# The loads of an exchange write every fourth partition instead of 32 neighbours, in a transformer block with expert routing

## The chip, the cores and the metric

The kernel runs on one core of one Trainium2 chip. Time is device time in microseconds (us) of the whole program on that core; smaller is better. A profile is one further execution, recorded by the hardware profiler.

## What is computed

The reference is one conditioned transformer block with expert-choice routing, in float32 throughout, for x of 16 sequences x 256 tokens x 256 features:

```python
shift = silu(t) @ W_ada.T + b_ada
h = ln(x, ln1_g, ln1_b) + shift
qkv = (h @ Wqkv.T).reshape(b, n, 3, H, HD)          # H = 16 heads, HD = 64
q = ln(qkv[:, :, 0].transpose(0, 2, 1, 3), qn_g, qn_b)
k = ln(qkv[:, :, 1].transpose(0, 2, 1, 3), kn_g, kn_b)
attn = softmax(einsum('bhnd,bhmd->bhnm', q, k) / sqrt(HD))
x = x + (attn @ v) @ Wout.T
gate = softmax(tok @ Wgate.T)                        # 4096 tokens, 8 experts
vals, idx = top_k(gate.T, 512)                       # each expert takes its 512 tokens
y = gelu(g @ fc1s + b1s) @ fc2s + b2s                # g: the tokens taken, layer-normed
tok = tok.at[idx].add(y * vals)
```

## The kernel before, in words

**Stages.** The program has an attention stage, in which the 16 sequences overlap like a pipeline (to about 800 us of the span), then a search for each expert's tokens, and then 16 expert jobs (8 experts, half of their tokens each). The change touches the attention stage alone.

**Order.** Each engine (TensorE = PE, VectorE = DVE, ScalarE = ACT, GpSimd = POOL, and the sync engine SP, which issues most DMAs) works through its own queue in order. The steps of the attention stage are declared with `plan.step` (lines 1330 to 1442), each with its engine, its assumed duration, what it needs and which buffers it holds. Their order does not come from those durations at build time: `plan.order(PLACES)` (line 1519) sorts them by a long list of places written out in the source (line 182). Semaphores then make each step wait for its data and its buffers.

**One sequence.** `First` norms the tokens and turns them into `hT`. `Group` (line 676) makes 512 columns of q, k or v for 128 tokens: `matmul` (688) into one of three PSUM buffers `pm`; for q and k `square` on ACT (701), `stats` on DVE (705), `power` on POOL (711 and 103), and `scale` on DVE (721), which empties `pm` into `qk` in SBUF. For v, ACT's `copy` (697) empties `pm`. `Quad` (line 796) does four heads, two at a time: `scores` (813) into two of four PSUM buffers `sc`, `maxima` on DVE (821), `exps` on ACT (830, one instruction for each 128 queries x 256 keys, with the row sum), `invert` on DVE (837), `normalise` on POOL (841), then the turned probabilities `prT` enter `product` (900), which ACT's `evict` (915) empties into `oT`. `Tail` (918) multiplies by Wout (926), adds x, stores, and computes the gates.

**The exchange.** q, k and the probabilities must be turned, so that what lay along the columns lies along the partitions. The first and the last sequence (`DIRECT`) do this with TensorE transposes. The other 14 do it in three steps. DVE transposes 32 x 32 blocks inside each group of 32 partitions (`turn`: line 754 for q and k into `kb`, line 851 for the probabilities into `pb`; two instructions of 128 x 512 fill one tile). SP then stores the whole tile of 512 KB to HBM in one DMA (`away`: 761 and 859). Last, SP loads it back in four DMAs of 128 KB (`back`: 773 and 873), each of which brings one 32-column block of all four partition groups to 32 partitions of the destination, in runs of 1 KB:

```python
for q in range(QB):                 # QB = 4, SQ = 32
    nc.sync.dma_start(
        prT[bass.ts(q, SQ)], self.blocks[i][:, :, q].rearrange("k m n -> m k n")
    )
```

So load q writes the 32 neighbouring partitions 32q to 32q + 31. For q and k, `affine` on ACT (781 and 789) then applies gain and bias. A sequence has 4 such round trips for q and k and 8 for the probabilities.

Of the kernel before, what the change touches and what calls it, by code (L numbers as in the profile page):

```python
# [12 lines left out]
AF = mybir.ActivationFunctionType  # L13
# [13 lines left out]
TB = N // P  # L27
# [7 lines left out]
SQ = 32  # L35
QB = P // SQ
# [28 lines left out]
def kernel(  # L65
# [105 lines left out]
    DIRECT = (0, B - 1)  # L171
# [356 lines left out]
    if True:  # L528
# [9 lines left out]
        xs, hTs, qTs, kTs, vs, oTs = {}, {}, {}, {}, {}, {}  # L538
# [134 lines left out]
        def plain(kT):  # L673
            return kT.rearrange("p g k t h m -> p (g k t h m)").rearrange("p (h n) -> p h n", n=N)

        class Group:
# [74 lines left out]
            def turn(self, kb):  # L751
                if self.t == 0:
                    kb.append(work.tile([P, QB, TB, HP // 2, SQ], F32, tag="pb", bufs=3, name="kb"))
                nc.vector.transpose(
                    kb[0][:, :, self.t],
                    self.qk.rearrange("p (h q d) -> p q h d", q=QB, d=SQ),
                )

            def away(self, kb):
# [6 lines left out]
            def back(self):  # L766
                if self.g < 2:
                    self.raw = work.tile([P, QB, TB, HP // 2, SQ], F32, tag="qraw", bufs=2, name="qraw")
                else:
                    self.raw = self.keys()[:, self.g - 2]  # L770
                raw = self.raw.rearrange("p k t h m -> p k (t h m)")
                for q in range(QB):
                    nc.sync.dma_start(
                        raw[bass.ts(q, SQ)], self.blocks[:, :, q].rearrange("k d n -> d k n")
                    )

            def affine(self):
# [18 lines left out]
        class Quad:  # L796
# [5 lines left out]
            def scores(self, i):  # L802
                hp = 2 * self.d + i
                direct = self.b in DIRECT
                keys = plain(kTs[self.b]) if direct else (
                    kTs[self.b].rearrange("p g k t h m -> p g h (k t) m")
                )
                for j in range(2):
                    self.sc[i, j] = ps.tile([P, TB, N], F32, tag="sc", bufs=4, name="sc")
                for t in range(TB):  # L810
                    for j in range(2):
                        rows = slice(j * HD, (j + 1) * HD)
                        nc.tensor.matmul(  # L813
                            self.sc[i, j][:, t, :], qTs[self.b][rows, hp, bass.ts(t, P)],
                            keys[rows, hp] if direct else keys[rows, hp // 4, hp % 4],
                            start=True, stop=True,
                        )
# [7 lines left out]
            def exps(self, i, j):  # L825
                if i not in self.sums:
                    self.sums[i] = stat.tile([P, 2, 2, TB], F32, tag="sums", name="sums")
                self.pr[i, j] = work.tile([P, TB, N], F32, tag="pr", bufs=PRB, name="pr")
                for t in range(TB):
                    nc.scalar.activation(  # L830
                        self.pr[i, j][:, t, :], self.sc[i, j][:, t, :], AF.Exp,
                        bias=self.nmax[i, j][:, t : t + 1], scale=1.0,
                        accum_out=self.sums[i][:, 0, j, t : t + 1],
                    )
# [34 lines left out]
            def back(self, i):  # L869

                prT = self.turned(i).rearrange("p (k n) -> p k n", k=QB)
                for q in range(QB):
                    nc.sync.dma_start(
                        prT[bass.ts(q, SQ)], self.blocks[i][:, :, q].rearrange("k m n -> m k n")
                    )

            def transposes(self, i, j):
# [472 lines left out]
        for b in range(B):  # L1350
# [16 lines left out]
            for (g, t), p in GROUP.items():  # L1367
                p += base
                a = Group(b, g, t)
                n = (b, g, t)  # L1370
# [27 lines left out]
            for d in range(HP // 2):  # L1398
                a = Quad(b, d)
                p = base + d * QUAD  # L1400
                g = d // 2
                n = (b, d)
                po = ("po", 0) + n
                for i in range(2):
                    q = p + 3 * i
                    m = n + (i,)
                    sums, pb, prT, blocks = ("sums",) + m, ("pb",) + m, ("prT",) + m, ("blocks",) + m
# [20 lines left out]
            for t in range(TB):  # L1428
                a = Tail(b, t)
                p = base + TAIL[t]  # L1430
                n = (b, t)
# [55 lines left out]
        for n in range(2):  # L1487
            a = jobs[n]
            k = top + 10 + 20 * n
# [19 lines left out]
        k = top + 30  # L1509
# [36 lines left out]
        for k in range(1, len(jobs)):  # L1546
# [4 lines left out]
            for s in range(SLOTS):  # L1551
# [28 lines left out]
                else:  # L1580
                    i, q = divmod(s - FC, 4)
# [56 lines left out]
```

## Time and profile before

| | us |
|---|---|
| median of 3 runs | 1095.7 (1095.66 to 1098.27) |
| the profiled execution | 1098.5, its span from first to last instruction 1096.8 |
| busy over the span | PE 1050.9 (96%), DVE 809.8 (74%), POOL 615.8 (56%), ACT 591.5 (54%) |
| busy from 100 to 750 us | PE 634.0, DVE 540.4, POOL 445.7, ACT 417.3, of 650 |
| DMA in the same stretch | 0.97 of the 16 DMA engines' time, 278 GB/s |

In the profile, L754 is line 754 of the kernel. A group of instructions is given as line, engine, operation, tile written <- tiles read, the shapes (partitions x elements), the number of instructions, then the busy time in us and the mean of one in ns, then the idle time that the engine had just before them and what ended it. A busy PE is not a PE at its peak, since the ends of matmuls are modelled; the spacing of their starts is the safer reading.

### The profile page before, as it was taken

How to read it: one execution, taken by the hardware profiler on the slowest of the kernel's cores; microseconds unless marked ns; L12 is line 12 of the kernel's file. 1: busy time of each engine (PE TensorE's matmuls, PEld its weight loads, DVE VectorE, ACT ScalarE, POOL GpSimd, SP SyncE). 2: the span in 40 equal slices, each digit the busy share in tenths (PEclk: the TensorE clock that was granted, in tenths of full speed). 3: DMA queues.
4: the chain of work that ended last, by engine and by line, in shares of the span. 5: the costliest groups of instructions: out<-in, count | busy, mean ns of one | idle time of the engine just before them, and what ended most of it. 6: DMA issues, size and time to landing. Idle time of an engine off the chain costs nothing. (4 is left out here: it accounts for less than half of the span.)

```text
span 1096.8 us, 18716 instructions
## 1 busy us (share of the span) xinstructions
PE 1050.9 (96%) x5611; PEld 685.9 (63%) x5611; DVE 809.8 (74%) x2257; ACT 591.5 (54%) x1656; POOL 615.8 (56%) x997
## 2 busy tenths in 40 slices
PE   6999999999999999999999999999988999999996
PEld 3555646556454645555565555656667888888885
DVE  6667878888887797887888788875579488655540
ACT  1768666666665655666666557675622323332331
POOL 3766766678667585666667676665411333333332
PEclk8999999999999999999999999999999999999998
DMA  6026989999998999998999999986120456565661
GB/s 213 1 77 188 273 261 294 285 281 261 282 278 269 282 280 284 283 286 255 281 294 275 285 283 266 310 265 186 64 101 20 132 172 202 169 174 171 194 202 19
DMA packets 167700, 238.56 MB, mean 218 GB/s; under 512 B 17328, under 2 KB 139440, under 8 KB 167600
## 3 DMA queue, kind: packets, MB, share of 16 engines
q1 hardware_dynamic: 159680, 227.08, 70.2%
q0 software_dynamic: 6144, 8.39, 4.2%
q10 hardware_dynamic: 1776, 1.90, 0.5%
q8 instruction: 45, 0.74, 0.3%
q14 instruction: 55, 0.45, 0.2%
HBM read 136.64 MB, written 100.66 MB: 216 GB/s over the span
## 5 line engine op out<-in xcount | busy, mean ns | idle before, releaser
L688 PE MATMUL pm<-wq,hT 128*128 128x512 f32 x768 | 361.5, 606 | 13.1 <-DVE qk L721 6.3
L841 POOL TENSOR_SCALAR pr<-pr,sums 128x256 f32<-128x256 f32 x512 | 237.0, 481 | 107.3 <-DVE sums L837 99.5
L830 ACT ACTIVATE pr<-sc,nmax 128x256 f32<-128x256 f32 x512 | 237.3, 481 | 98.3 <-DVE nmax L821 78.6
L688 PEld LDWEIGHTS pm<-wq,hT 128*128 128x128 f32 x768 | 136.8, 190 | 168.1 <-issue 131.6
L103 POOL TENSOR_TENSOR ss<-ss,neghalf 128x8 f32<-128x8 f32 x128 | 211.0, 1648 | 10.6
L821 DVE TENSOR_REDUCE nmax<-sc 128x2 f32<-128x512 f32 x256 | 165.4, 673 | 19.9 <-PE sc L813 19.6
L851 DVE STREAM_TRANSPOSE pb<-pr 128x512 f32<-128x512 f32 x224 | 150.1, 690 | 20.7 <-DMA kblocks<-kb 9.5
L813 PE MATMUL sc<-kT,qT 64*128 64x256 f32 x1024 | 137.4, 396 | 3.5 <-ACT kT L789 3.0
L900 PE MATMUL po<-prT,v 128*64 128x256 f32 x1024 | 129.5, 387 | 2.1 <-DMA prT<-blocks 1.8
L701 ACT ACTIVATE sq<-pm 128x512 f32<-128x512 f32 x128 | 75.8, 604 | 96.1 <-PE pm L688 95.6
L813 PEld LDWEIGHTS sc<-kT,qT 64*128 64x128 f32 x1024 | 91.9, 186 | 52.8 <-issue 26.7
L1319 POOL DMA_INDIRECT out<-y,idx x32 | 51.2, 1599 | 119.1 <-DVE y L1313 65.9
L1286 PE MATMUL ph<-xT,w 128*128 128x256 f32 x512 | 117.8, 383 | 0.0
L1302 PE MATMUL py<-w,hid 128*128 128x256 f32 x512 | 116.3, 380 | 0.0
L926 PE MATMUL pw<-wo,oT 128*128 128x256 f32 x512 | 115.3, 382 | 0.0
L926 PEld LDWEIGHTS pw<-wo,oT 128*128 128x128 f32 x512 | 96.2, 190 | 20.9 <-issue 6.0
L830 ACT ACTIVATION_READ_ACCUMULATOR pr<-sc,nmax 128x1 f32 x512 | 109.0, 213 | 0.0
L900 PEld LDWEIGHTS po<-prT,v 128*64 128x64 f32 x1024 | 66.8, 136 | 67.1 <-issue 23.7
L705 DVE TENSOR_REDUCE ss<-sq 128x8 f32<-128x512 f32 x128 | 85.1, 671 | 29.1 <-ACT sq L701 28.6
L1293 ACT ACTIVATE hid<-ph,vec 128x256 f32<-128x256 f32 x128 | 60.3, 473 | 84.6 <-PE ph L1286 79.5
L1302 PEld LDWEIGHTS py<-w,hid 128*128 128x128 f32 x512 | 95.6, 190 | 12.8
L1286 PEld LDWEIGHTS ph<-xT,w 128*128 128x128 f32 x512 | 95.4, 190 | 12.8
(141 smaller groups left out, 1096.1 us busy)
## 6 DMA issues: line engine op xcount, KB each, us to landing
blocks<-pb SPq DMA_DIRECT2D x112, 512.0 KB, 5.0
prT<-blocks SPq DMA_DIRECT2D x448, 128.0 KB, 4.3
kblocks<-kb SPq DMA_DIRECT2D x56, 512.0 KB, 4.3
w<-in_fc2T SPq DMA_DIRECT2D x16, 1024.0 KB, 5.7
w<-in_fc1T SPq DMA_DIRECT2D x16, 1024.0 KB, 8.3
qraw<-kblocks SPq DMA_DIRECT2D x112, 128.0 KB, 4.0
kT<-kblocks SPq DMA_DIRECT2D x112, 128.0 KB, 4.2
out<-tok SPq DMA_DIRECT2D x32, 128.0 KB, 4.1
```

What stands on the lines that cost most here:

```text
L103: nc.gpsimd.tensor_tensor(dst, src, neghalf[:, : src.shape[1]], ALU.pow)
L688: nc.tensor.matmul(self.pm, hTs[self.b][:, c, bass.ts(self.t, P)], wq[:, c, bass.ts(self.g, GW)], start=(c == 0), stop=(c == DC - 1),)
L705: nc.vector.tensor_reduce(self.ss[:, 0, :], self.sq.rearrange("p (h d) -> p h d", d=HD), AX.X, ALU.add,)
L813: nc.tensor.matmul(self.sc[i, j][:, t, :], qTs[self.b][rows, hp, bass.ts(t, P)], keys[rows, hp] if direct else keys[rows, hp // 4, hp % 4] ...
L821: nc.vector.tensor_reduce(self.nmax[i, j], self.sc[i, j], AX.X, ALU.max, negate=True)
L830: nc.scalar.activation(self.pr[i, j][:, t, :], self.sc[i, j][:, t, :], AF.Exp, bias=self.nmax[i, j][:, t : t + 1], scale=1.0, accum_out=se ...
L841: nc.gpsimd.tensor_scalar(self.pr[i, j][:, t, :], self.pr[i, j][:, t, :], self.sums[i][:, 1, j, t : t + 1], 1.0, ALU.mult, ALU.mult,)
L851: nc.vector.transpose(self.pb[i][:, :, :, j].rearrange("p k c t n -> p t k c n"), self.pr[i, j].rearrange("p t (k c m) -> p t k c m", c=TB ...
L900: nc.tensor.matmul(self.po[j * HD : (j + 1) * HD, i, :], vs[self.b][:, c, bass.ts(4 * self.d + 2 * i + j, HD)], prT[:, j, c] if self.b in ...
L926: nc.tensor.matmul(self.pw, oTs[self.b][:, hp // 2, self.t, hp % 2, :], wo[:, hp, :], start=(hp == 0), stop=(hp == HP - 1),)
L1286: nc.tensor.matmul(self.ph[f], self.w1[:, c, bass.ts(f, P)], self.xT[:, c, :], start=(c == 0), stop=(c == DC - 1),)
L1302: nc.tensor.matmul(self.py[i], self.hid[:, f, bass.ts(i, P)], self.w2[:, f, :], start=(f == 0), stop=(f == FC - 1),)
```

## The change

Load q writes partitions q, q + 4, q + 8, ... q + 124. For the data to land where it did, block q must hold every fourth column instead of 32 neighbouring ones. For q and k, DVE's transpose (754) reads its source with a step of four elements, 16 bytes. For the probabilities, ACT's exponential reads the scores from PSUM with that step and writes them to SBUF in block order without gaps, so that `normalise` and DVE's transpose (851) are as before. The matmul of the scores now takes the keys in their natural order, still in runs of 32 neighbouring elements. The DIRECT sequences, the stores, the number, sizes and queues of the DMAs, and the order of every queue are as before.

```diff
@@ Group.turn
                 nc.vector.transpose(
                     kb[0][:, :, self.t],
-                    self.qk.rearrange("p (h q d) -> p q h d", q=QB, d=SQ),
+                    self.qk.rearrange("p (h d q) -> p q h d", q=QB, d=SQ),
                 )
@@ Group.back
                     nc.sync.dma_start(
-                        raw[bass.ts(q, SQ)], self.blocks[:, :, q].rearrange("k d n -> d k n")
+                        raw[q::QB], self.blocks[:, :, q].rearrange("k d n -> d k n")
                     )
@@ Quad.scores
                 keys = plain(kTs[self.b]) if direct else (
-                    kTs[self.b].rearrange("p g k t h m -> p g h (k t) m")
+                    kTs[self.b].rearrange("p g k t h m -> p g h t k m")
                 )
@@ Quad.exps
                 for t in range(TB):
+                    dst, src = self.pr[i, j][:, t, :], self.sc[i, j][:, t, :]
+                    if not (self.b in DIRECT):
+                        dst = dst.rearrange("p (q c m) -> p q c m", q=QB, c=TB)
+                        src = src.rearrange("p (c m q) -> p q c m", q=QB, c=TB)
                     nc.scalar.activation(
-                        self.pr[i, j][:, t, :], self.sc[i, j][:, t, :], AF.Exp,
+                        dst, src, AF.Exp,
@@ Quad.back
                     nc.sync.dma_start(
-                        prT[bass.ts(q, SQ)], self.blocks[i][:, :, q].rearrange("k m n -> m k n")
+                        prT[q::QB], self.blocks[i][:, :, q].rearrange("k m n -> m k n")
                     )
```

## The prediction

> **What bounds it now.** I read the busy times by stretch first, then TensorE's own waits, then the DMA. From 100 to 750 us the attention stage runs evenly:
>
> ```profile
> core 0: us, PE busy (x) PEld busy (x) DVE busy (x) ACT busy (x) POOL busy (x), PEclk, DMA share, GB/s
> 100.00:750.00 650.00, 633.98 (x3069) 360.00 (x3069) 540.39 (x1077) 417.34 (x1248) 445.70 (x773) 1.00 0.97 278
> ```
>
> Two things look full: PE (98%) and the DMA engines (0.97). DVE is at 83%, ACT at 64%. As a busy PE may be a waiting one, I took the spacing of matmul starts in the trace and counted what exceeds the usual spacing of each pair of lines. Stalls of over 0.15 us sum to 18.2 us from 100 to 770 us. So PE bounds the stage, and whatever speeds up everything else can win some 18 us. Following each stall back through its releases, 11 of the 25, worth 8.0 us, begin at the landing of a DMA. The rest come from DVE's and ACT's queues. PE's waits in that stretch show the same pattern:
>
> ```profile
> engine line waited for: us in total, times, longest us
> PE pm L688 <- DVE qk L721: 3.1, 6, 1.0
> PE sc L813 <- ACT kT L789: 3.0, 3, 1.9
> PE pm L688 <- ACT v L697: 2.8, 2, 1.6
> ...
> PE po L900 <- DMA prT<-blocks: 1.8, 3, 1.4
> ```
>
> The product waits for its loads (L900) only 1.8 us in all. DMA is full, but PE hardly feels it.
>
> **What the loads cost now.** A stretch with stores only, then one with loads only, then stores again:
>
> ```profile
> 404.75:405.75 1.00, 1.00 (x6) 0.90 (x5) 1.00 (x2) 1.00 (x5) 0.92 (x2) 1.00 0.94 345
> ...
> 406.50:409.75 3.25, 3.25 (x14) 1.86 (x14) 3.04 (x9) 1.52 (x2) 3.07 (x8) 1.00 1.10 225
> 410.75:411.75 1.00, 0.00 (x0) 0.00 (x0) 0.84 (x2) 0.69 (x1) 0.70 (x2) 1.00 1.04 375
> ```
>
> The last two columns are DMA share and GB/s: loads move 225, stores 345 to 375, both with all engines busy. In the packet records of the loads a 1 KB packet takes mostly 70 to 90 ns, while undisturbed ones take 46. So something makes the loads wait on each other, and 32 neighbouring partitions are a plausible something. Had every 1 KB packet its 46 ns, then from 300 to 350 us (7004 of them, 468 us over 16 engines, 29.2 us each) an engine would spend 20.1 us: 9 of 50 us are freed, a DMA share near 0.8. One load of four has 512 packets, 32 an engine; at 34 ns less each it lands 1.1 us sooner.
>
> **Gain.** If each of the 11 stalls shrinks by up to 1.1 us, 6.8 of the 8.0 us go. I take **-7 us**. What is late next is the queues of DVE and ACT, whose stalls (10 us) stay.
>
> **Costs.** Nothing is reordered, and no DMA or wait is added: the queues hold the same steps, so nothing moves past another. Two kinds of instruction get a 16-byte step in what they read:
>
> ```profile
> L830 ACT ACTIVATE pr<-sc,nmax 128x256 f32<-128x256 f32 x512 | 237.3, 481 | 98.3 <-DVE nmax L821 78.6 <-POOL pr L841 8.3 <-POOL ss L103 5.6
> ...
> L754 DVE STREAM_TRANSPOSE kb<-qk 128x512 f32<-128x512 f32 x112 | 77.6, 697 | 6.5 <-DMA blocks<-pb 5.6
> ...
> L1172 DVE TENSOR_SCALAR partf<-pplace 128x256 f32<-128x256 f32 x2 | 0.9, 426 | 4.1 <-PE pplace L1161 4.1
> ...
> L998 DVE TENSOR_TENSOR gate_of<-gates,smax 128x224 f32<-128x224 f32 x1 | 0.7, 744 | 0.0
> ...
> L1034 DVE COPY gates<-pgT 128x256 f32<-128x256 f32 x1 | 0.4, 414 | 0.0
> ...
> L990 DVE TENSOR_TENSOR gates<-gates,smax 128x224 f32<-128x224 f32 x1 | 0.4, 392 | 0.0
> ```
>
> The trace has no read at 16 bytes. The nearest rows bracket it. L1172 writes with a step of 8 bytes and takes 426 ns, against 414 for the gapless copy L1034: free. L998 writes with a step of 128 bytes: 744, against 392 for L990 of the same form, so 1.57 ns more for each of 224 elements. So an element costs 0 to 1.57 ns more, and both rows are writes of DVE; for ACT's read of PSUM they are a distant bound. A gain is excluded: the same elements go through. I take one cycle of DVE, 1.03 ns (from 679 ns for the 512 elements of L721 and 415 for the 256 of L933), and as much for ACT by its own pace (0.83 ns, from 594 for 512 and 380 for 256 in its copies). This is a choice near the middle, not a measurement.
>
> DVE: a transpose goes from 697 to about 1230 ns, 112 x 0.53 = 59 us. ACT: an exponential goes from 481 to about 694, 448 (14 sequences) x 0.213 = 95 us. From 100 to 750 us (102 and 448 of them) DVE would be busy 540 + 54 = 594 of 650 us (91%), ACT 513 (79%). Neither passes PE, so most of it is hidden under the matmuls. But the queues are in order: behind a late transpose stand `scale` (L721), which frees PE's `pm`, and `maxima` (L821), for which ACT and then PE's `sc` wait. For the share that reaches PE I followed the releases back from PE's last work before 765 us to 100 us by the rule of the chain of waits (the page's own chain ends at once in POOL's queue). On that path lie 357 us of PE, 127 of DMA, 93 of DVE, 29 of ACT. L754 has 11.3 us there, 16% of its transposes, and the exponentials 11.8 us, 5.5% of theirs. Present shares give 59 x 0.16 + 95 x 0.055 = 9.5 + 5.2 us. As DVE's idle time halves (110 to 56 us) and ACT's falls from 233 to 137, delays are absorbed less: shares of 33% and 9.5% give 19.6 + 9.1 us. I take the middle, **+15 and +7 us**.
>
> The Trainium skill bears on this choice: "SBUF — State Buffer", section "Door 1: The DMA port swizzle", says that SBUF is read at full rate only with at least two hits in each 16-byte line, and that PSUM's lines are 8 bytes. The rows L1172 (8 bytes, two hits) and L998 (one) agree. By it a 16-byte step is slowed on both engines, which speaks against the change; without a slowdown the sum would be the -7 alone.
>
> At nothing: the scores' new key order. Its inner runs are 32 elements before and after, and the DIRECT sequences, which read keys without gaps, have the same 376 ns median of L813. If it did cost, PE would show it at once: 896 matmuls, 0.01 us each is 9 us. The exponential still writes without gaps, so `normalise` and the 224 transposes of L851 stay at 481 and 690 ns.
>
> **Sum.** -7 + 15 + 7 = +15 us. On the profiled execution's 1098.5 us (span 1096.8, with 1.7 around it) that is 1113.5; it lies 2.8 above the median, so for the median **1111 us**.
>
> **Rivals.**
>
> *Strided reads are free* (0 ns an element, as at 8 bytes). Then only the gain is left: 1089, at best 1084 if some stalls in DVE's queue came from the DMA too, at worst 1092. For it: L1172. Against it: L998.
>
> *DVE becomes the bound.* At 1.57 ns an element the transposes take 1.5 us: 540 + 102 x 0.80 = 622 of 650 us, and ACT 417 + 448 x 0.40 = 597. DVE now waits 110 us, 27 of it for DMAs; if the other 83 stay, it needs 705 us, PE starves for `pm`, and the stage is 55 us longer: 1151. It decides once DVE's work and the waits it can't lose pass 650 us, that is beyond about 0.27 us more for each transpose if none of those 83 us can be lost, and beyond 1.1 us if all can. Against it: much of DVE's waiting is slack that a later DVE simply uses up.
>
> *It cancels*: only one engine is slowed, or the loss hides under PE, and the sooner loads pay for the rest: 1093 to 1098.
>
> *The change doesn't do what it says*: engines still meet in pairs at the same place, since each writes two of the 32 partitions in turn, and loads stay near 225 GB/s. With the slow reads that is +22 us, 1118; it lies inside the forecast's range.
>
> **How the numbers follow.** Forecast (slow reads, partly hidden; with or without quicker loads), 1099 to 1135: 50%. Free reads: 25%. Cancelled: 14%. DVE the bound, 1135 to 1175: 11%. A measurement here can tell 0.3%, 3.3 us, from no change. Faster takes the free reads, 25%; no change 14%; slower 61%. The range from 1088 to 1142 leaves out the lowest third of the free reads' times and most of the DVE-bound case. The forecast's own is 1099 to 1135.
>
> **What would show it.** L754's mean: 1230 ns right, 700 wrong, 1500 for the DVE-bound rival; L830's: 690 against 481. Loads-only stretches above 300 GB/s, 1 KB packets near 46 ns and a DMA share near 0.8 show the gain's cause. PE's waits for L721, L697 and L830 should grow, and those for kT and prT shrink. The prediction is wrong if the strided rows keep their time, or if they slow and PE's stalls stay at 18 us.

## The result, and the profile after

The changed kernel takes 1134.4 us (median of 4 runs, 1132.9 to 1136.0), the kernel before 1095.7 on the same chip: a ratio of 1.034, with a 95% interval from 1.032 to 1.036. It is slower by 3.4%, some 37 us, where +15 us had been forecast. One of the runs further below, of `e2_qk_only`, took 2129 us, is counted as slow, and is left out of its ratio.

Three groups and a queue of the profile page after come first. The columns of a group are line, engine, operation, tiles, shapes and count, then busy us and mean ns of one, then idle us before it and what ended most of it. Below 830 the line numbers have moved by four: L834 was L830, L855 was L851, L877 was L873.

```profile
q1 hardware_dynamic: 159680, 227.08, 59.6%
...
L834 ACT ACTIVATE pr<-sc,nmax 128x256 f32<-128x256 f32 x512 | 237.6, 481 | 125.0 <-DVE nmax L821 101.9
...
L855 DVE STREAM_TRANSPOSE pb<-pr 128x512 f32<-128x512 f32 x224 | 150.0, 691 | 27.0 <-DMA kblocks<-kb 10.2
...
L754 DVE STREAM_TRANSPOSE kb<-qk 128x512 f32<-128x512 f32 x112 | 123.3, 1105 | 5.4 <-DMA blocks<-pb 4.7
```

DVE's strided transpose went from 697 to 1105 ns. ACT's strided exponential did not move at all: 481 before, 481 after. The queue q1 carried the same 159680 packets and 227 MB in 59.6% of the DMA engines' time, against 70.2% before:

```profile
q1 hardware_dynamic: 159680, 227.08, 70.2%
```

The stretch from 100 to 750 us, with two shorter stretches from inside it, by the view of busy times (the last three columns are granted clock, DMA share and GB/s):

```profile
100.00:750.00 650.00, 613.84 (x2898) 345.13 (x2897) 551.77 (x1028) 393.93 (x1173) 422.54 (x732) 0.99 0.79 265
343.00:351.00 8.00, 6.57 (x26) 3.10 (x27) 6.72 (x14) 4.58 (x13) 3.62 (x4) 0.79 0.75 226
422.50:424.50 2.00, 2.00 (x11) 1.74 (x11) 2.00 (x6) 1.99 (x6) 1.62 (x2) 1.00 0.77 202
```

Every engine but DVE is busy for less of it than before (PE 614 against 634), and DVE is at 552 of 650: none of the five is full any more. The DMA share fell from 0.97 to 0.79, as forecast. But the third line is a stretch with loads only, and they move 202 GB/s, less than the 225 of before, at a share of 0.77. Now it isn't the packets that are slow: for a quarter of that stretch the DMA engines have nothing to do. The stretch is a usual one: over all stretches of 1.5 us or more without a packet of 2 KB or larger, from 100 to 750 us, the median is 227 GB/s at a share of 0.98 before (66 stretches), and 208 at 0.69 after (72).

The last matmul of Wout (L930 after) starts at 843.4 us instead of 808.8; what follows takes 288 to 289 us in both. So the whole loss, 34.6 us between the two profiled executions, lies in the attention stage. Counted as the prediction counted them, PE's stalls there rose from 18.2 us (25 of them) to 47.1 (54). What PE waits for is a new list (100 to 780 us):

```profile
engine line waited for: us in total, times, longest us
PE pl L967 <- ACT oT L919: 12.0, 5, 3.9
PE po L904 <- DMA prT<-blocks: 5.1, 4, 2.3
PE pm L688 <- DVE qk L721: 4.7, 8, 1.1
PE pm L688 <- ACT hT L659: 3.3, 1, 3.3
```

The first row is the tail of a sequence. Its gates (L967) wait behind the last evicted product, and a product waits for its loads. Its stalls are few and long: 12 us in five.

The view that explains them is SP's own instructions: duration in ns, min/median/max of one DMA issue. First before, then after:

```profile
L873 SPq DMA_DIRECT2D prT<-blocks x440: 302/430/1713, 105.0 to 747.4; - x147
```

```profile
L877 SPq DMA_DIRECT2D prT<-blocks x408: 577/602/1812, 106.1 to 748.5; - x136
L773 SPq DMA_DIRECT2D qraw<-kblocks x104: 577/602/1262, 109.4 to 743.9; - x104
```

Issuing one stepped load holds SP's queue for 602 ns, where a load to neighbours took 302 at best and 430 in the median. From the start of one load to the start of the next of the same four, the median is 0.647 us instead of 0.48. SP issues DMAs for 514 of the 650 us (79%), against 410 (63%) before. And 131072 bytes every 0.647 us are 203 GB/s: the stretch of loads alone showed 202.

### The profile page after: what moved, and what is told of

It reads as the page before. It is cut to its first block, busy times and chain, and to the rows that moved or that the text cites. A ratio compares the mean times of both kernels' runs of the same rounds, so it can differ in the third digit from the quotient of the medians.

```text
span 1131.5 us, 18747 instructions
## 1 busy us (share of the span) xinstructions
PE 1062.7 (94%) x5611; PEld 689.8 (61%) x5611; DVE 849.4 (75%) x2257; ACT 591.7 (52%) x1656; POOL 617.0 (55%) x997
## 3 DMA queue, kind: packets, MB, share of 16 engines
q1 hardware_dynamic: 159680, 227.08, 59.6%
## 5 line engine op out<-in xcount | busy, mean ns | idle before, releaser
L688 PE MATMUL pm<-wq,hT 128*128 128x512 f32 x768 | 366.2, 611 | 18.9 <-DVE qk L721 7.9
L834 ACT ACTIVATE pr<-sc,nmax 128x256 f32<-128x256 f32 x512 | 237.6, 481 | 125.0 <-DVE nmax L821 101.9
L855 DVE STREAM_TRANSPOSE pb<-pr 128x512 f32<-128x512 f32 x224 | 150.0, 691 | 27.0 <-DMA kblocks<-kb 10.2
L813 PE MATMUL sc<-kT,qT 64*128 64x256 f32 x1024 | 140.8, 398 | 2.7 <-ACT kT L789 2.1
L754 DVE STREAM_TRANSPOSE kb<-qk 128x512 f32<-128x512 f32 x112 | 123.3, 1105 | 5.4 <-DMA blocks<-pb 4.7
L930 PE MATMUL pw<-wo,oT 128*128 128x256 f32 x512 | 115.3, 382 | 0.3 <-DVE qk L721 0.3
L930 PEld LDWEIGHTS pw<-wo,oT 128*128 128x128 f32 x512 | 96.2, 190 | 21.2 <-issue 4.9
L834 ACT ACTIVATION_READ_ACCUMULATOR pr<-sc,nmax 128x1 f32 x512 | 108.2, 211 | 0.0
```

The costliest lines, as they stand in the source:

```text
L688: nc.tensor.matmul(self.pm, hTs[self.b][:, c, bass.ts(self.t, P)], wq[:, c, bass.ts(self.g, GW)], start=(c == 0), stop=(c == DC - 1),)
L754: nc.vector.transpose(kb[0][:, :, self.t], self.qk.rearrange("p (h d q) -> p q h d", q=QB, d=SQ),)
L813: nc.tensor.matmul(self.sc[i, j][:, t, :], qTs[self.b][rows, hp, bass.ts(t, P)], keys[rows, hp] if direct else keys[rows, hp // 4, hp % 4] ...
L834: nc.scalar.activation(dst, src, AF.Exp, bias=self.nmax[i, j][:, t : t + 1], scale=1.0, accum_out=self.sums[i][:, 0, j, t : t + 1],)
L855: nc.vector.transpose(self.pb[i][:, :, :, j].rearrange("p k c t n -> p t k c n"), self.pr[i, j].rearrange("p t (k c m) -> p t k c m", c=TB ...
L930: nc.tensor.matmul(self.pw, oTs[self.b][:, hp // 2, self.t, hp % 2, :], wo[:, hp, :], start=(hp == 0), stop=(hp == HP - 1),)
```

## The experiments

Each ratio is to the kernel before on the same chip; "us" behind it is that ratio on 1095.7 us. In the first four, two theories stood against each other. **Q**: the loss is DVE's slower transposes, late in an in-order queue. I believed this one first, since following PE's last work back through the releases put 235 of 698 us on DVE, against 93 of 665 before. **L**: the loss comes with the stepped loads. The last four set **S** (issuing a stepped load holds SP's queue longer) against what was left of L.

**Only the probabilities' half of the change** (`e1_probs_only`): q and k are turned and loaded as before.

```diff
 # against the changed kernel
-                    self.qk.rearrange("p (h d q) -> p q h d", q=QB, d=SQ),
+                    self.qk.rearrange("p (h q d) -> p q h d", q=QB, d=SQ),
...
-                        raw[q::QB], self.blocks[:, :, q].rearrange("k d n -> d k n")
+                        raw[bass.ts(q, SQ)], self.blocks[:, :, q].rearrange("k d n -> d k n")
```

> The changed kernel with the q/k part undone: line 754 reads neighbours again and its loads write 32 neighbours; the probabilities keep the strided exponentials and the spread loads. Theory Q (the loss is DVE's 112 strided transposes, 46 us of DVE time, which an in-order queue hands on to PE almost whole): the loss is gone and the sooner loads are left, 1088 to 1096 us, L754 back at about 700 ns. Rival L (the loss comes from the loads landing sooner in an order written for slower ones, or from the probabilities' new path): slower than before by 10 us or more, 1106 to 1130.

Measured: 1115.1 us, ratio 1.014 (1.012 to 1.016), +15 us. No instruction of DVE is strided here, and 448 of the 672 loads are stepped. By Q there should have been no loss.

**Only the q and k half** (`e2_qk_only`): the two edits above, made the other way round in the kernel before.

> The kernel before with only the q/k part of the change: strided transposes at line 754 and spread q/k loads; the probabilities as before. Theory Q: nearly the whole loss, with less of the loads' relief, 1128 to 1142 us. Rival L: most of the loss is missing, 1096 to 1112.

Measured: 1110.2 us, ratio 1.009 (1.006 to 1.012), +10 us. The whole of DVE's slow work is in this kernel, with 224 stepped loads, and together they cost a quarter of the loss. The two halves make 15 + 10 = 25 us apart and 37 together, so the cost is not in proportion to the number of loads; the row at the end of this section takes that up.

**The stepped loads alone** (`e3_loads_alone`): nothing is read with a step; only the destinations change.

```diff
 # against the kernel before
-                        raw[bass.ts(q, SQ)], self.blocks[:, :, q].rearrange("k d n -> d k n")
+                        raw[q::QB], self.blocks[:, :, q].rearrange("k d n -> d k n")
...
-                        prT[bass.ts(q, SQ)], self.blocks[i][:, :, q].rearrange("k m n -> m k n")
+                        prT[q::QB], self.blocks[i][:, :, q].rearrange("k m n -> m k n")
```

> The kernel before with only the loads spread over every fourth partition and no strided read; so the rows of q, k and the probabilities land in the wrong partitions, while every instruction has its usual size. Theory Q: faster by what the stalls that begin at a landing hold, at most 8 us: 1088 to 1095. Rival L: slower, 1105 to 1130.

Measured: 1127.6 us, ratio 1.026 (1.024 to 1.029), +29 us. The busy view of this kernel:

```profile
100.00:750.00 650.00, 617.40 (x2908) 347.33 (x2910) 518.11 (x1034) 397.20 (x1179) 424.50 (x735) 0.98 0.79 266
```

DVE is the least loaded of all versions so far (518 of 650), DMA is at 0.79, and the kernel is 29 us slower. So Q falls as the explanation of the whole.

**The strided reads alone** (`e4_strides_alone`): the same two lines, put back in the changed kernel.

> The changed kernel with its strided reads but the loads to 32 neighbours as before; so rows land in the wrong partitions. Theory Q: the loss without the relief, 1134 to 1150 us. Rival L: near the kernel before, 1096 to 1112.

Measured: 1108.2 us, ratio 1.008 (1.006 to 1.010), +9 us. With 29 from the loads that makes 38, against 37 for the change: the two parts add up.

**Each exchange loaded by one DMA** (`e5_one_load`). With the step, the 128 destination partitions run through the four blocks in one regular order, so the four loads can be one of 512 KB.

```diff
 # against the changed kernel
-                for q in range(QB):
-                    nc.sync.dma_start(
-                        prT[q::QB], self.blocks[i][:, :, q].rearrange("k m n -> m k n")
-                    )
+                nc.sync.dma_start(prT, self.blocks[i].rearrange("k m q n -> (m q) k n"))
 # and the same for raw
```

> The changed kernel with each four loads of an exchange joined in one DMA: with every fourth column in a block, 128 partitions in their order are one source step in HBM, so one load of 512 KB does what four of 128 KB did. Theory S (a load to every fourth partition holds SP's queue for 602 ns at the median instead of 430, 0.17 us more for each of 672, and the in-order queue hands that on): SP's issuing falls from 514 us (100 to 750 us) to under 200, the loads' loss goes, and only the strided transposes' 9 us is left, less what sooner loads can win: 1094 to 1108 us. Rival L (loads that land sooner upset the rest, or take something from the engines): still 1120 to 1140 us, as the loads land sooner still.

Measured: 1091.1 us, ratio 0.997 (0.996 to 0.998), -3.5 us, below even the 1094 to 1108 that S expected: SP's queue is freer now than it was before the change. The same bytes land in the same places, DVE's transposes are as slow as in the change, and the loss is gone. SP's issues and the largest of SP's waits, in this kernel:

```profile
L873 SPq DMA_DIRECT2D prT<-blocks x111: 359/374/1330, 106.8 to 745.5; - x111
```

```profile
SPq L860 <- DVE pb L852: 120.4, 64, 6.8
```

One load of 128 partitions is issued in 374 ns, where a quarter of it took 602. SP issues for 170 of 650 us and spends most of the rest waiting for DVE's data; before and in the change its largest waits were for the probabilities' stores to land:

```profile
SPq L873 <- DMA blocks<-pb: 65.4, 44, 5.3
SPq L877 <- DMA blocks<-pb: 26.2, 16, 3.8
```

In the change steps whose data was ready stood behind SP's issues, and the traces show it directly. Taken in order, each store of the probabilities belongs to two transposes of DVE. From the end of the second one to the issue of the store, the median of the 112 is 1.2 us before, 2.6 in the change, 2.8 in `e3_loads_alone` and 0.03 here. The same loads-only reading in this kernel, from 424.25 to 428.50 us:

```profile
424.25:428.50 4.25, 4.25 (x14) 1.97 (x12) 3.51 (x7) 2.27 (x6) 2.98 (x7) 1.00 0.95 291
```

291 GB/s at a share of 0.95, now that the engines get their work in time. It is one of the fuller ones: the median of all such stretches in this kernel is 240 GB/s at 0.79.

**The same, and the step moved to a read of PSUM** (`e6_one_load_psum`): `scale` reads `pm` with the step and writes `qk` gapless in block order; the transpose then reads without a step.

```diff
 # against the changed kernel, besides the edit of the one load
                 engine.tensor_tensor(
-                    self.qk.rearrange("p (h d) -> p h d", d=HD),
-                    src.rearrange("p (h d) -> p h d", d=HD),
-                    self.ss[:, 1, :].unsqueeze(2).to_broadcast([P, 8, HD]), ALU.mult,
+                    self.qk.rearrange("p (q h d) -> p q h d", q=QB, h=8),
+                    src.rearrange("p (h d q) -> p q h d", q=QB, h=8),
+                    self.ss[:, 1, :].unsqueeze(1).unsqueeze(3).to_broadcast([P, QB, 8, HD // QB]),
+                    ALU.mult,
                 )
...
-                    self.qk.rearrange("p (h d q) -> p q h d", q=QB, d=SQ),
+                    self.qk.rearrange("p (q h d) -> p q h d", q=QB, d=SQ),
```

> As the one with joined loads, and the strided read moved from DVE's transpose (L754, SBUF) to DVE's scaling (L721), which reads the matmul's result in PSUM in block order and writes without gaps. If DVE reads PSUM with a 16-byte step as freely as ACT did, L721 stays at 680 ns and L754 goes back to 700: theory S says 1085 to 1096 us, below the kernel before; rival L 1112 to 1132. If DVE pays in PSUM as in SBUF (about 0.4 us), it equals the one with joined loads, 1094 to 1108.

Measured: 1078.3 us, ratio 0.985 (0.983 to 0.986), -17 us: faster than both kernels, and below the 1085 to 1096 expected. DVE's groups and the busy view of it:

```profile
L762 DVE STREAM_TRANSPOSE kb<-qk 128x512 f32<-128x512 f32 x112 | 77.2, 694 | 0.8
L728 DVE TENSOR_TENSOR qk<-pm,ss 128x512 f32<-128x512 f32 x112 | 75.8, 679 | 16.2 <-POOL ss L103 14.5
```

```profile
100.00:750.00 650.00, 650.00 (x3198) 374.39 (x3195) 551.48 (x1100) 430.94 (x1275) 454.81 (x789) 1.00 0.82 282
```

The transpose is back at 694 ns, and `scale`, which now reads PSUM with a step of 16 bytes, takes the 679 that it took without one. PE is busy in all 650 us. By the count of stalls over 0.15 us it has none. The 17 us won are nearly the 18.2 us of PE's stalls that the prediction called the most there was to win.

**Does the step make the issue long, or the busier queue?** (`e7_steps`): in the kernel before, q's loads write every second partition of 64, k's every fourth, and the probabilities' stay at neighbours.

```diff
 # against the kernel before
+                    two = bass.ds(q // 2 * 64, 64)
+                    dst = raw[two][q % 2 :: 2] if self.g < 2 else raw[q::QB]
                     nc.sync.dma_start(
-                        raw[bass.ts(q, SQ)], self.blocks[:, :, q].rearrange("k d n -> d k n")
+                        dst, self.blocks[:, :, q].rearrange("k d n -> d k n")
                     )
```

> The kernel before with other destinations of the q and k loads: q every second partition of 64, k every fourth of 128, the probabilities still 32 neighbours; q and k rows land in wrong partitions. One look, for the time that SP's queue is held by each kind of issue. Theory S: k loads about 602 ns at the median and the probabilities 430 in the same run; q shows whether any step costs this or only the fourth. Rival: all three kinds take the same, so that the longer issues belong to a busier queue and not to the step. Time near 1105 to 1112 us.

Measured, in one execution: 1098.6 us. Before's own profiled execution, on another chip, took 1098.5, and ten runs of before on this chip 1092.6 to 1097.0, with a median of 1094.6; so 0 to 4 us for 224 stepped loads, less than the 1105 to 1112 expected. SP's issues, all in one execution:

```profile
L775 SPq DMA_DIRECT2D qraw<-kblocks x104: 572/602/1753, 107.7 to 709.5; - x104
L775 SPq DMA_DIRECT2D kT<-kblocks x104: 577/604/1927, 112.3 to 717.5; - x104
L875 SPq DMA_DIRECT2D prT<-blocks x440: 302/430/1740, 105.1 to 747.6; - x147
```

On one queue, mixed together, the stepped ones take 602 and 604 and the others 430. It is the step, of two as of four, and not the load on the queue.

**A longer issue without any step** (`e8_sp_drains`): the kernel before, with an instruction on SP behind each load that only holds its queue, four times.

```diff
 # against the kernel before, after each of the two loads
+                    for _ in range(4):
+                        nc.sync.drain()
```

> The kernel before with four drain instructions in SP's queue after each of the 672 loads, and nothing else changed, to hold the queue longer while every transfer stays as it was. Theory S: if the four hold SP for about as long as the step of four partitions did (0.17 us), the time rises by 15 to 35 us, to 1113 to 1134; if they hold it for 0.05 us, by 3 to 10. Rival L: no change, whatever they hold, 1095 to 1101.

Measured: 1138.6 us, ratio 1.041 (1.039 to 1.043), +44 us, above the 1113 to 1134 expected. The four held SP for 0.21 us a load by the spacing (0.69 against 0.48), more than the step's 0.17. A store of the probabilities now stands 3.0 us in the median behind its data. With the data, the work of DVE and ACT, and the destinations all as before, delay in SP's queue alone makes the loss of the change and more.

The runs make a row: extra time on SP's queue against time lost. Extra is 0.167 us for each stepped load, 0.21 for each load with drains.

| kernel | loads lengthened | extra on SP, us | lost, us |
|---|---|---|---|
| `e7_steps` | 224 | 37 | 0 to 4 |
| `e1_probs_only` | 448 | 75 | 15 |
| `e3_loads_alone` | 672 | 112 | 29 |
| `e8_sp_drains` | 672 | 141 | 44 |

The first 40 us or so vanish in SP's idle time. Of what comes on top, a third to a half reaches the end. The row mixes number with kind: the 224 are all q's and k's loads, the 448 all the probabilities'. The first three kernels also have the destinations that make packets quicker, and `e8_sp_drains` has not. These were not separated. Nor did I try one load for the kernel before: with neighbours, the source of a joined load needs one dimension more.

## Why the prediction was wrong, point by point

**The step that failed** is the sentence "Nothing is reordered, and no DMA or wait is added: the queues hold the same steps". It holds for order and number. But it passes off each of the 672 loads as the same instruction, with no price for the issue itself, which is 0.17 us longer. On SP's in-order queue that is 112 us, in a queue that was issuing for 63% of the stage and waited at its head for stores to land for another 65 us, by SP's waits. The cost is +29 us (e3), with the step as the cause of the long issue (e7) and the long issue as a sufficient cause of the loss (e8), and it goes when the issues go (e5). The prediction gave a price to DVE and ACT, and none to the queue that the edit itself was in. Yet the path that it followed back from PE's last work holds 18.6 us of SP's queue before, which it did not list beside PE, DMA, DVE and ACT; in the change it is 39.6. A row to bound the cost was there, too: the trace of before has issues of one form of load from 302 to 1713 ns, with 430 in the median, so 672 loads at 0.1 us more, 67 us, would have raised the question of what SP's idle time can absorb.

**DVE's transposes**: forecast 1230 ns and +15 us. Measured 1105 ns (0.80 ns more an element, from 408 ns over 512), and +9 us in e4. With SP relieved, e5 against e6, taking the stride away is worth 13 us. The slow read was right, and its price a little high. (The larger of its two shares comes to 31 to 32% by its own numbers, 16% x 110 / 56, and not 33%; that takes half a microsecond off the 15.)

**ACT's exponentials**: forecast 694 ns and +7 us. Measured 481 ns and nothing. The choice "near the middle" of 0 and 1.57 ns was wrong: two rows of DVE's writes to SBUF said nothing of a read of PSUM. The Trainium skill ("SBUF — State Buffer", section "Door 1: The DMA port swizzle") has lines of 16 bytes for SBUF, with two hits in a line needed for full rate, and lines of 8 bytes for PSUM, where it speaks of matmuls alone. The transpose agrees with it. The prediction carried the rule over to what engines read from PSUM, and the exponential (481 and 481) and `scale` in e6 (679 and 679) do not follow it: neither ACT nor DVE lost anything with a step of 16 bytes in PSUM.

**The quicker loads**: the signs came, and the cause is only in part shown. 1 KB packets take 46 ns in the median and 53 in the mean (from 300 to 350 us; 67 in the mean before), the DMA share is 0.79 for "near 0.8", and a load of the probabilities lands 3.1 us after its issue instead of 4.3, 1.2 us sooner for the 1.1 worked out (that is the sum for the four loads of a tile, which have 512 packets; one load has 128). These are the page's rows, with KB and us to landing, first the probabilities' before and then after:

```profile
prT<-blocks SPq DMA_DIRECT2D x448, 128.0 KB, 4.3
```

```profile
prT<-blocks SPq DMA_DIRECT2D x448, 128.0 KB, 3.1
...
qraw<-kblocks SPq DMA_DIRECT2D x112, 128.0 KB, 3.0
kT<-kblocks SPq DMA_DIRECT2D x112, 128.0 KB, 3.3
```

But e8, whose loads go to 32 neighbours and are only issued more slowly, shows much of the same: packets of 46 ns in the median and 57 in the mean, and a DMA share of 0.83. So a part of the relief is the slower pace itself. That the destination counts too is seen in e5, where SP's issuing no longer sets the pace, the destination is all 128 partitions, and a full stretch of loads still moves 291 GB/s, against 225 before, with packets of 46 and 52 ns.

And landing is counted from the issue, while the fourth issue now comes 3 x 0.167 = 0.5 us later, behind every other delay of the queue. The sign "loads-only stretches above 300 GB/s" failed for the same reason: 202, the pace of issuing. From 100 to 750 us PE's wait for `prT`, which was to shrink, went from 1.8 to 3.4 us. The -7 us never stood alone in a run. From e4 to e5, which makes the loads both quick and few, the gain is 12 us.

The Trainium skill would have led the same way as I went: "DMA: Bandwidth & Descriptors", section "Issuing engines are not separate DMA queues", calls the time to initiate a DMA "usually small relative to the DMA itself". For one load that is so (0.6 of 3.1 us). For four of them in a row on one queue, 2.6 us, it is not, and here it decided the time.

**The rivals.** Free strided reads: half true, for PSUM, and not for SBUF. DVE as the bound: false, DVE is at 85% (552 of 650) and PE does 20 us less in the same time. Cancelled: false, by 37 us. Loads that stay near 225 GB/s: by their number they did stay, but at a share of 0.77 and by the pace of issuing, not because engines met. The measured time lies inside the stated range, at the upper end of the forecast's own case, for another reason than the one that the range was drawn from; that is luck.

## What to carry to other kernels

A DMA that is made quicker in the engines can be dearer in the queue that issues it: before changing a DMA's pattern, read the issue durations and the issuing engine's share of the stage, as for any other engine. When stalls end on a DMA, look whether the queue stood waiting for its data (then data is late) or the data waited for the queue (then the queue is). And if a pattern makes several DMAs one regular walk, join them: here that, with the strided read put where it is free, turned +37 us into -17.

## What the runs showed of the hardware that was not expected

- A load whose destination steps over partitions, by two or by four, is issued in 602 to 604 ns (median), one to 32 neighbours in 430 (302 at best), and one to all 128 in 374. Why is not settled: the trace shows the duration, not its parts.
- A read of PSUM with a step of 16 bytes is free for ACT (481 ns for 256 elements, both ways) and for DVE (679 ns for 512, both ways); DVE's transpose from SBUF with that step pays 0.80 ns an element.
- Long gaps of PE can cost twice. After the gap of 3.05 us in the timeline of PE after, the same four matmuls that took 1.96 us before take 2.80, and the granted clock of that stretch is 0.79 (second line of the busy view above):

```profile
340.25 1.13 PE L813 MATMUL sc<-kT,qT 64*128 64x256 f32 x8
344.43 0.61 PE L967 MATMUL pl<-wg,tokT 128*128 128x8 f32 x4 [3.05 <-ACT oT L919]
344.89 2.80 PE L688 MATMUL pm<-wq,hT 128*128 128x512 f32 x4
```

  In the clock record after, three stretches of the attention stage from 100 us on (13.6 us in all) run at half clock, and before none; so at most 6.8 of the 34.6 us are this. In e8 such stretches sum to 34 us and in e3 to 24, so up to 17 of the 44 us lost by the one and 12 of the 29 by the other; e5 and e6 have none there. Some stops of PE are thus paid a second time, and this may be a part of why the row of the experiments rises faster than in proportion; no run separates it. A gap of 3.3 us at 695 us was followed by none, so the length of the gap alone does not decide it.
